# A graph attention kernel: seven row tiles are transposed by DMA as half words instead of by TensorE, and the search steps over adj are placed differently

## The chip, the core and the metric

The kernel runs on one core of a Trainium2 chip. The time is device microseconds (us) of one execution of the whole program. A core has a matrix engine (TensorE, in the profile PE; its weight loads are PEld), three engines for element work (VectorE = DVE, ScalarE = ACT, GpSimd = POOL), a sync engine (SP) whose work here is to issue DMAs, and 16 DMA engines that all queues share. Each engine works through its own list of instructions in order and waits on semaphores for the others.

## What is computed

One layer of attention over a graph of 2708 nodes with 1024 features, in float32. `adj` is a matrix of zeros and ones with a one at a chance of 0.0014771, so that a node has four neighbours on average.

```python
h = jnp.maximum(_layernorm(x, axis=-1), 0.0)
q = h @ W_q.T + b_q;  k = h @ W_k.T + b_k;  v = h @ W_v.T + b_v
z = scale * (q @ k.T) * adj
z = jnp.where(z == 0.0, -10000.0, z)
out = x + relu(softmax(z, axis=1) @ v)
```

## The kernel before

**What is multiplied.** The kernel never forms k or v. It folds W_q and W_k into one matrix M, makes rows q = h M + bias, fetches for each node the rows h of its neighbours, takes scores as dot products of q with them, and adds the neighbours' rows up, weighted by the softmax: u. Then out = x + relu(u W_v + b_v). So there are two large products, both of 128 rows by 1024 with 1024x1024: h by M ("q units") and u by W_v ("o units").

**Row tiles.** There are 22 tiles of 128 rows, the last with 20. Rows are sorted by their number of neighbours, in two parts: tiles 0 to 10, and 11 to 21. The sort needs the lists of neighbours ("keys") of all rows of its part, and it yields a table (`tab`) by which rows are scattered and gathered from then on.

**The search for neighbours.** A tile of adj (128x2708, 1354 KB) is loaded by SP (L317) into one of three buffers, tile t into buffer t % 3. ACT passes over it once (`counted`, L324, output `sized`) to sum it, which is a check value; DVE searches it for the positions of the ones (`found`, L334, four or five instructions over 128x685 or less), and then makes the list of keys from the positions (`listed`, L346 to L352), one time per batch of up to four tiles. Tiles 20 and 21 are batches of their own. The next tile for a buffer can load when both ACT's pass and DVE's search of the tile before are through. The search steps stand between the matmul blocks, in a table `steps_at` that maps (unit, position) to a string: `p` is ACT's pass alone, `f` is search and, at a batch's end, list, `i` is search alone, `j` is list alone, `e` is all of them. `c` stands for the counts of a part, `o` for its sort. The counts of the second part stand at unit 3, position 2, its sort at unit 3, position 3 (L604 `hot` on DVE, then two small matmuls at L615 and L617).

**A unit.** A unit is a pair of tiles, multiplied with seven block products in place of eight, of sums of quarter blocks: per unit the operands a11, a12 (of the first tile), a22, a21 (of the second), and sums s1 to s4 of them, against quarters of M (or W_v) and their sums T. A block is four matmuls of 128x512 in `add_block` (L909). In `multiply` the blocks come in the order s2, a12, s4, s3, then a11 and s1 of the **next** unit (`opened`), then a22; `after(0)` to `after(6)` run what stands between them. The sums that are c12, c22 (p or q rows, L1020 for o units) are made on DVE from PSUM, c11 and c21 on ACT. Units n = 0 to 9 are q pairs; n = 10 to 19 are o pairs: (8,7), (6,5), (4,3), (2,0), (1,9), (15,14), (13,12), (16,17), (20,10), (18,19). Tile 11 is left over and is multiplied alone at the end.

**How a row tile comes to stand as an operand.** The features must lie on the partitions, so each 128x1024 tile is transposed. `half_turned` (L357 to L360) has PE transpose four blocks of 128x128 into one PSUM bank `pt`, twice a tile. `blocks` (L640 to L680) has ACT copy a11, a12 and a22 out of PSUM (L649) and DVE make s1 and s3 from a21 in PSUM, s2 and s4 from SBUF (L653). In `after`, the first tile of the next pair is turned at position 0 and the second at position 2. For tile 11, `turned` (L362 to L367) does the same into one tile `T_alone`.

**The attention stream.** From unit 5 on, `attention` runs as a stream of steps beside the matmuls, `advance(share)` after each block: scores of the next tile on DVE (L790, 128x1024 with a sum), exp on ACT (L806), coefficients on DVE (L834), the first product coef times g on ACT (L835), the other products added on DVE one after another (`sums`, L843). The rows g are gathered by POOL (L545). The order of tiles is 8, 7, 6, 5, 4, 3, 2, 0, 1, 9, 15, 14, 13, 12, 16, 17, 20, 10, 18, 19, 11. Tiles 10 and 20 hold nodes without neighbours and take a row sum of h besides. If two tiles' neighbours fit together (`ahead`), two score steps of the next tile come ahead of a tile's weights. The finished u either stays in SBUF (`held`, when it is used within two units) or is stored by POOL to `u_dram`, from where SP loads it again (`load_rows`, L1103) two units ahead of its use.

**What sets the order.** DVE's order is written out by hand throughout, ACT's and POOL's by hand up to unit 5 and by the compiler's scheduler after that; SP's queue takes adj loads, row loads, weights for the o units and small tail transfers in their order.

Of the kernel before, what the change touches and what calls it, by code (L numbers as in the profile page):

```python
# [10 lines left out]
FT = mybir.dt.float32  # L11
U32 = mybir.dt.uint32
I32 = mybir.dt.int32
U16 = mybir.dt.uint16
AF = mybir.ActivationFunctionType
ALU = mybir.AluOpType
AX = mybir.AxisListType

P = 128
NB = 512  # L20
# [12 lines left out]
FAR = 20.0  # L33
WIDE = 8
LIGHT = 4
ROOT = 32
BATCHES = ((0, 3), (4, 7), (8, 11), (12, 15), (16, 19), (20, 20), (21, 21))

# [19 lines left out]
def tile_preln_masked_attention(  # L58
# [12 lines left out]
    nc = tc.nc  # L71
    N, D = x.shape
    DC = D // P
# [4 lines left out]
    FULL = N // P  # L78
# [4 lines left out]
    K = slot_counts(EARLY * P, EARLY) + slot_counts(N - EARLY * P, FULL - EARLY) + [0]  # L83
# [7 lines left out]
    dram = ctx.enter_context(tc.tile_pool(name="dram", bufs=1, space=bass.MemoryType.DRAM))  # L91
# [3 lines left out]
    q_dram = dram.tile([EARLY * P, D], FT, name="q_dram")  # L95
    q_late = dram.tile([(FULL - EARLY) * P, D], FT, name="q_late")
    u_dram = dram.tile([FULL * P, D], FT, name="u_dram")
    m_dram = dram.tile([2, 2, P, 4, NB], FT, name="m_dram")
    tv_dram = dram.tile([4, P, 4, NB], FT, name="tv_dram")
    bp_dram = dram.tile([1, D], FT, name="bp_dram")  # L100
# [54 lines left out]
    t = 0  # L155
    while t < NT:
# [4 lines left out]
        t = e  # L161
# [24 lines left out]
    def row_tile(name):  # L186
        return work.tile([P, D], FT, tag="row", name=name, bufs=ROWS)
# [166 lines left out]
    def half_turned(xt, s):  # L354

        pt = psum.tile([P, 4, P], FT, tag="tp", name="pt")
        for c in range(4):  # L357
            k = s * 4 + c
            nc.tensor.transpose(pt[:, c, :], xt[:, k * P:(k + 1) * P], ident)  # L359
        return pt  # L360

    def turned(xt, name):  # L362

        hT = work.tile([P, D], FT, tag="hT", name=f"T_{name}", bufs=2).rearrange("p (c q) -> p c q", q=P)
        for s in range(DC // 4):
            nc.scalar.copy(hT[:, s * 4:(s + 1) * 4, :], half_turned(xt, s))
        return hT  # L367

    ordered = ExitStack()
    ordered.enter_context(tc.manual_schedule(engines={mybir.EngineType.Activation, mybir.EngineType.DVE}))  # L370
# [17 lines left out]
    with tc.tile_pool(name="w", bufs=1, side="left") as wp:  # L388
# [73 lines left out]
        if True:  # L462
# [7 lines left out]
            for o in range(DC):  # L470
# [6 lines left out]
                else:  # L477
                    k = o - H
# [60 lines left out]
    def small(name):  # L539
        return half.tile([P, NB], FT, tag="half", name=name, bufs=14)  # L540
# [98 lines left out]

    behind = []  # L640

    def blocks(xa, xb, eng=None):


        ops = {}

        def held(name, bank):
            ops[name] = small(name).rearrange("p (c q) -> p c q", q=P)
            nc.scalar.copy(ops[name], bank)  # L649

        def put(name, a, b, op, eng=None):
            ops[name] = small(name).rearrange("p (c q) -> p c q", q=P)
            step = (eng or nc.vector).tensor_tensor(ops[name], a, b, op=op)  # L653
            if eng is None:
                behind.append(step)

        def upper():
            held("a11", half_turned(xa, 0))
            held("a12", half_turned(xa, 1))

        def lower():
            held("a22", half_turned(xb, 1))
            a21 = half_turned(xb, 0)
            put("s1", ops["a22"], a21, ALU.add)
            put("s3", ops["a11"], a21, ALU.subtract)
            put("s2", ops["s1"], ops["a11"], ALU.subtract, eng)
            put("s4", ops["a12"], ops["s2"], ALU.subtract, eng)

        return ops, upper, lower
# [3 lines left out]
    def banks_for(row):  # L673

        return_ = []
        for h in range(NH):
            return_.append(psum.tile([P, NB], FT, tag="acc", name=f"ps{h}"))
            nc.scalar.copy(return_[h], row[:, h * NB:(h + 1) * NB])
        return return_

    def natural_rows(n):
# [15 lines left out]
    nc.vector.tensor_scalar(large[:, 0:1], large[:, 0:1], 10000.0, None, op0=ALU.is_gt)  # L697
    nc.vector.tensor_scalar(large[:, 1:2], large[:, 1:2], 250000.0 / D, None, op0=ALU.is_gt)

    steps_at = {(0, 0): "s4-5 e9", (0, 1): "r4 +0 +1 +2 f10", (0, 3): "p10 i11", (0, 4): "j11 a4 p11", (0, 5): "h4 +3 s6-7 e12",  # L700
# [3 lines left out]
    steps_ahead = {(2, 2): "o s10"}  # L704

    slots, free = [], []
# [132 lines left out]
    def sums(t):  # L839
        u, coef = us.pop(t)  # L840
        for s in range(0 if t in EMPTY else 1, K[t]):
            fill()
            chained(lambda: nc.vector.scalar_tensor_tensor(  # L843
                u, g_of[t][s], coef[:, at[t][s]:at[t][s] + 1], u, op0=ALU.mult, op1=ALU.add))
            free.append(g_of[t][s])
            yield 1.3
        fill()
        g_of.pop(t)
        if near(t):
            held[t] = u  # L850
        else:
            nc.gpsimd.dma_start(u_dram[t * P:(t + 1) * P, :], u)
        done.add(t)

    def attention(order):
        for t in order[:2]:
            ask(t)

        fill()
        yield 0.0  # L860
        with tc.issue_after(chain[-1].ins):
            for lo, hi in parts:
                nc.vector.tensor_scalar(valid[:, lo:hi], ptab.bitcast(U32)[:, lo:hi, 0:SLOTS], float(N) - 0.5, NONE,
                                        op0=ALU.is_lt, op1=ALU.max)
        free.extend(slots[:8])
        fill()
        yield 0.0
        fetch(order[0])
        after = order[1:] + [None, None]
        yield from scores(order[0], after[0])  # L870
        for i, t in enumerate(order):
            nxt = after[i]
            ahead = nxt is not None and K[t] + K[nxt] <= HIGH + 1
            part = scores(nxt, after[i + 1]) if nxt is not None else iter(())
            if ahead:

                for _ in range(2):
                    yield next(part, 0.0)
            weights(t)
            yield 0.6  # L880
            if ahead:
                yield from part
            yield from sums(t)
            yield from part
# [9 lines left out]
    def near(t):  # L894

        return t == alone or any(t in unit[1:] for unit in units[:now[0] + 3] if unit[0] == "o")
# [190 lines left out]
    o_pairs = [(order[i], order[i + 1]) for i in range(0, FULL - 1, 2)]  # L1087
    alone = order[-1]
    units = [("q",) + p for p in q_pairs] + [("o",) + p for p in o_pairs]

    def load_rows(unit):
        kind, *pair = unit
        rows = []
        for t in pair:
            if t in held:
                rows.append(held.pop(t))
                continue
            rows.append(row_tile(f"{kind}r_{t}"))
            if kind == "q":
                gather(rows[-1], h_dram[:, :], t, SLOTS, P)  # L1100
            else:
                assert t in done, (t, done)
                nc.sync.dma_start(rows[-1], u_dram[t * P:(t + 1) * P, :])  # L1103
        return rows
# [42 lines left out]
    for n, unit in enumerate(units):  # L1147
# [10 lines left out]
        def after(i):  # L1158
# [18 lines left out]
            if nxt is not None:  # L1177

                if n == FIRST - 1 and i in (0, 2):
                    single_turned(i // 2)  # L1180
                if i == (3 if n in (0, FIRST - 1) else 0):
                    ops_of[n + 1] = blocks(*rows_of[n + 1], nc.gpsimd if n + 1 < FIRST - 1 else None)
                    if n != FIRST - 1:
                        ops_of[n + 1][1]()
                if n != FIRST - 1 and i == (4 if n == 0 else 2):
                    ops_of[n + 1][2]()
                    rows_of.pop(n + 1)
                    if n == last_q - 1:
                        all_rows()
                if i == 3:  # L1190
                    if n == FIRST - 1:
                        single["banks"] = banks_for(bp_sb)
                    else:
                        banks_of[n + 1] = banks_for(bp_sb)
                if i == 4 and n + 2 < FIRST:
                    natural_rows(n + 2)
                if i == (2 if n == FIRST else 4) and n + 2 >= FIRST and n + 2 < len(units) and n + 2 not in rows_of:
                    while units[n + 2][0] == "o" and not done.issuperset(units[n + 2][1:]):
                        advance(1.0)
                    rows_of[n + 2] = load_rows(units[n + 2])  # L1200
# [6 lines left out]
            if nxt is None and i == 1:  # L1207
                while alone not in done:
                    advance(1.0)
                r, = load_rows(("o", alone))  # L1210
                single["turned"] = turned(r, "alone")
            if nxt is None and i == 3:
                single["banks"] = banks_for(bp_sb)
            if n == last_q - 1 and i == 4:

                nc.sync.dma_start(bp_sb, bv.to_broadcast([P, D]))
                nc.vector.tensor_sub(bp_sb[:, NB:], bp_sb[:, NB:], bp_sb[:, :NB])
# [238 lines left out]
```

## Time and profile before

| | |
|---|---|
| median of 3 runs | 669.54 us (668.49 to 670.58) |
| profiled execution, its own time | 670.24 us |
| its span, first to last instruction | 668.4 us |
| granted TensorE clock, mean | 0.993 |
| ACT busy | 264.3 us, 40% |
| POOL busy | 401.4 us, 60% |
| share of the chain that ended last: PE | 79% |
| the same: DMA 5%, DVE 5%, POOL 4%, ACT 2%, issue 5% | |
| gathers of rows g (L545), 104 of them | 125.1 us of POOL |
| scores (L790), 92 | 112.6 us of DVE, 1.22 us each |
| sums (L843), 77 | 98.8 us of DVE, 1.28 us each |
| ACT's passes over adj (L324), 22 | 54.2 us, 2.46 us each |
| ACT's copies out of the transposes (L649), 60 | 33.2 us |
| DMA, 193.24 MB | mean 289 GB/s over the span |

A line of PE, DVE or ACT in a timeline gives the start and the duration in us, the engine, the line of the kernel, the operation, output<-input, shapes, and the number of instructions in a row; in square brackets stands the idle time of the engine just ahead and what ended it. A line of the waits gives engine and tile, the engine and tile that ended the wait, then the sum in us, the count, and the mean. Matmuls of one group overlap: the distance from one group's start to the next one's is what a group costs, 3.43 us for a block of four matmuls that shows 3.60 us in its line.

### The profile page before, as it was taken

To read this page: it belongs to the slowest core of one execution; us is meant where nothing else is said; L and a number is where in the kernel's file an instruction comes from. 1 tells how busy PE (TensorE), PEld (TensorE's weight loads), DVE (VectorE), ACT (ScalarE), POOL (GpSimd) and SP (SyncE) were. 2 spreads that over 40 slices of the span, in tenths; PEclk is the share of its full clock that TensorE was granted. 3 is DMA by queue.
4 is the path that set the end of the run, shared out by engine and by line. 5 is a ranking of instruction groups with operands and counts; after the bars stand their busy time and mean duration, and the time that the engine had idled before them with its cause. 6 is when DMAs were issued, how large, how long until landed. Compare 5 with 4: busy or idle time off the path is not lost.

```text
span 668.4 us, 6383 instructions
## 1 busy us (share of the span) xinstructions
PE 653.6 (98%) x1768; PEld 334.0 (50%) x1768; DVE 526.0 (79%) x1014; ACT 264.3 (40%) x395; POOL 401.4 (60%) x396
## 2 busy tenths in 40 slices
PE   7999999999998999999999999999999999999994
PEld 4777766444543444444444444444444444444441
DVE  5999879999887403988887999798798989989221
ACT  3467985765654212332241232432332433322200
POOL 2559991666476763775656365574674877873331
PEclk9999999999998999999999999999999999999998
DMA  8997989599575996897899999998997799895631
GB/s 345 408 360 259 371 302 377 220 400 340 207 222 171 343 374 219 276 393 240 312 312 351 382 417 390 305 302 252 325 299 193 235 296 364 220 278 170 147 121 66
DMA packets 62164, 193.24 MB, mean 289 GB/s; under 512 B 9689, under 2 KB 10041, under 8 KB 61226
## 3 DMA queue, kind: packets, MB, share of 16 engines
q0 software_dynamic: 34464, 109.25, 49.8%
q1 hardware_dynamic: 26650, 80.37, 32.5%
q10 hardware_dynamic: 1008, 3.15, 1.2%
q8 instruction: 16, 0.26, 0.2%
q14 instruction: 26, 0.21, 0.1%
HBM read 160.85 MB, written 44.93 MB: 308 GB/s over the span
## 4 chain that ended last, share of the span: by engine, by line
PE 79%; issue 5%; DMA 5%; DVE 5%; POOL 4%; ACT 2%; POOLq 0%; SPq 0%; DVEq 0%; ACTq 0%
PE ps L909 35%; PE psy L909 24%; PE ps_y L418 6%; PE ps_x L418 4%; PE ps_z L418 4%; PE pt L359 4%; POOL g L545 2%; DMA out_dram<-y,tab 2%; DMA adj<-in_adj_dram 2%; DVE junk L790 1%; DVE at L334 1%; POOL y L1008 1%; ACT sized L324 1%; DVE u L843 1%; DMA wlow<-in_wq_dram 1%
## 5 line engine op out<-in xcount | busy, mean ns | idle before, releaser
L545 POOL DMA_INDIRECT g<-h_dram,tab x104 | 125.1, 1203 | 54.5 <-issue 22.5
L909 PE MATMUL ps<-M,a 128*128 128x512 f32 x320 | 144.1, 593 | 0.1
L909 PE MATMUL psy<-wlow,s 128*128 128x512 f32 x320 | 144.1, 592 | 0.0
L790 DVE SCALAR_TENSOR_TENSOR junk<-g,pq 128x1024 uint8<-128x1024 f32 x92 | 112.6, 1224 | 2.3 <-DMA g<-h_dram,tab 0.4
L843 DVE SCALAR_TENSOR_TENSOR u<-g,coef,u 128x1024 f32<-128x1024 f32 x77 | 98.8, 1283 | 8.9 <-ACT u L835 7.3
L909 PEld LDWEIGHTS ps<-M,a 128*128 128x128 f32 x320 | 59.3, 190 | 68.0 <-issue 67.2
L909 PEld LDWEIGHTS psy<-wlow,s 128*128 128x128 f32 x320 | 59.2, 190 | 67.2 <-issue 67.2
L334 DVE FIND_INDEX8 at<-ones,adj 128x8 uint32<-128x685 f32 (+1 forms) x88 | 74.4, 866 | 0.0
L909 PE MATMUL ps<-M,s 128*128 128x512 f32 x160 | 73.6, 603 | 0.0
L909 PE MATMUL psy<-wlow,a 128*128 128x512 f32 x160 | 72.1, 593 | 0.4 <-DVE p L1020 0.4
L909 PE MATMUL ps<-wlow,s 128*128 128x512 f32 x160 | 71.9, 592 | 0.0
L324 ACT ACTIVATE sized<-adj 128x2708 uint8<-128x2708 f32 (+1 forms) x22 | 54.2, 2463 | 5.1 <-DMA adj<-in_adj_dram 5.0
L909 PEld LDWEIGHTS ps<-M,s 128*128 128x128 f32 x160 | 30.9, 194 | 38.4 <-issue 38.4
L1008 POOL DMA_INDIRECT y<-in_x_dram,tab x19 | 34.0, 1788 | 26.7 <-ACT y L1025 14.9
L909 PEld LDWEIGHTS psy<-wlow,a 128*128 128x128 f32 x160 | 30.2, 190 | 39.2 <-issue 34.6
L909 PEld LDWEIGHTS ps<-wlow,s 128*128 128x128 f32 x160 | 30.4, 190 | 38.3 <-issue 38.3
L259 POOL TENSOR_TENSOR hsum<-hsum,x 128x1024 f32<-128x1024 f32 (+1 forms) x17 | 40.3, 2370 | 0.3
L653 DVE TENSOR_TENSOR s<-a,pt 128x512 f32<-128x512 f32 x40 | 25.6, 681 | 15.5 <-ACT a L649 6.9
L649 ACT COPY a<-pt 128x512 f32<-128x512 f32 x60 | 33.2, 593 | 9.5 <-remote 3.7
L547 POOL DMA_INDIRECT pq<-q_dram,tab x11 | 14.6, 1329 | 33.5 <-DVE junk L790 16.3
L744 POOL DMA_INDIRECT out_dram<-y,tab x21 | 24.9, 1186 | 15.4 <-DMA y<-in_x_dram,tab 7.7
L545 POOL DMA_INDIRECT M<-h_dram,tab x20 | 27.0, 1350 | 10.1 <-issue 4.9
(236 smaller groups left out, 887.1 us busy)
## 6 DMA issues: line engine op xcount, KB each, us to landing
adj<-in_adj_dram SPq DMA_DIRECT2D x21, 1354.0 KB
x<-in_x_dram SPq DMA_DIRECT2D x21, 512.0 KB
h_dram<-x POOLq DMA_DIRECT2D x21, 512.0 KB
u_dram<-u POOLq DMA_DIRECT2D x14, 512.0 KB
or<-u_dram SPq DMA_DIRECT2D x14, 512.0 KB
q_late<-q SPq DMA_DIRECT2D x10, 512.0 KB
pq<-q_late POOLq DMA_DIRECT2D x10, 512.0 KB
g<-in_wv_dram SPq DMA_DIRECT2D x16, 256.0 KB
```

The source lines that it names most:

```text
L259: nc.gpsimd.tensor_add(hsum[:n], hsum[:n], xt[:n])
L324: nc.scalar.activation(sized[:n], a[:n, :, :PW], AF.Abs, accum_out=total[:n, t:t + 1])
L334: nc.vector.max_index(at[:n, t - first_t, g, :], ones[:n, 0:8], a[:n, g, :])
L359: nc.tensor.transpose(pt[:, c, :], xt[:, k * P:(k + 1) * P], ident)
L418: mm = nc.tensor.matmul(bank, a_tile(o + H * a[0], a[1], i), b(o), start=first and o == 0, stop=(o == H - 1), skip_group_check=True)
L545: return nc.gpsimd.indirect_dma_start(out=dst, out_offset=None, in_=src, in_offset=off, bounds_check=N - 1, oob_is_err=False)
L649: nc.scalar.copy(ops[name], bank)
L653: step = (eng or nc.vector).tensor_tensor(ops[name], a, b, op=op)
L790: chained(lambda: nc.vector.scalar_tensor_tensor(junk, g_of[t][s], 1.0, tq[t], op0=ALU.mult, op1=ALU.mult, accum_out=zall[:, t, s:s + 1]))
L843: chained(lambda: nc.vector.scalar_tensor_tensor(u, g_of[t][s], coef[:, at[t][s]:at[t][s] + 1], u, op0=ALU.mult, op1=ALU.add))
L909: mm = nc.tensor.matmul(bank, a[:, c, :], b[:, c, :], start=False, stop=(c == 3), skip_group_check=True)
L1008: return nc.gpsimd.indirect_dma_start(out=y[:n], out_offset=None, in_=x, in_offset=off, compute_op=ALU.add)
```

## The change

Three things are done.

**Seven row tiles are no longer transposed on PE.** `TURNED = 3` names the last three o pairs, and with the tile left over they are the tiles 16, 17, 20, 10, 18, 19 and 11 (`turning`). The DMA transposes elements of two bytes, and the rows are float32, so a tile is first split: at the end of `sums`, ACT copies the high and the low half words of u, taken as 128x2048 numbers of 16 bits, into the two halves of a new row tile. It is held (16, 17, 10, 11) or stored by POOL in a new `u_split` (20, 18, 19). In `load_rows`, SP issues one transposing DMA for such a tile, in place of taking the held tile or loading from `u_dram`; it gives sixteen blocks of 128x128 half words. In `blocks_turned`, which stands for `blocks`, ACT joins high and low half words again into a11, a12, a22 and now a21 too, two copies for each, and DVE makes s1 to s4 all from SBUF. For these pairs the first tile is joined at position 3 of the unit before and the second at position 4, where they were turned at 0 and 2. For tile 11 the transposing DMA is issued in the last unit at position 1, and joined at position 4 into `T_alone`.

**Search steps are moved.** ACT's passes over the adj tiles 16, 17 and 18 each stand a step earlier; the search of 19 stands one step earlier and its list by itself behind it; the list of batch 8 to 11 stands one step later.

**A bound on the score steps.** `ahead` takes at most one step less than the next tile has scores, where it took two.

```diff
+TURNED = 3
+    u_split = dram.tile([FULL * P, 2 * D], U16, name="u_split")
...
+    def words_joined(dst, turned, lo, hi):
+        words = dst.bitcast(U16).rearrange("p (k w) -> p k w", w=2)
+        for w in (1, 0):
+            nc.scalar.copy(words[:, :, w], turned[:, (1 - w) * D + lo:(1 - w) * D + hi])
+    def blocks_turned(ta, tb):
...
+        def joined_half(name, turned, s):
+            half = small(name)
+            words_joined(half, turned, s * NB, (s + 1) * NB)
...
+        def upper():
+            joined_half("a11", ta, 0)
+            joined_half("a12", ta, 1)
+        def lower():
+            joined_half("a22", tb, 1)
+            joined_half("a21", tb, 0)
+            put("s1", "a22", "a21", ALU.add)
+            put("s3", "a11", "a21", ALU.subtract)
+            put("s2", "s1", "a11", ALU.subtract)
+            put("s4", "a12", "s2", ALU.subtract)
...
-    steps_at = {... (0, 3): "p10 i11", (0, 4): "j11 a4 p11", (0, 5): "h4 +3 s6-7 e12",
+    steps_at = {... (0, 3): "p10 i11", (0, 4): "a4 p11", (0, 5): "j11 h4 +3 s6-7 e12",
-                (1, 6): "f16 c", (2, 1): "f17", (2, 2): "p16 a8", (2, 3): "r10 f18 p17 w h8",
-                (2, 4): "a10 p18", (2, 5): "f19 k10", ...
+                (1, 6): "f16 c p16", (2, 1): "f17", (2, 2): "p17 a8", (2, 3): "r10 f18 p18 w h8",
+                (2, 4): "i19 a10", (2, 5): "j19 k10", ...
...
@@ in sums(t), behind the last sum @@
+        kept_in = u_dram
+        if t in turning:
+            words = u.bitcast(U16).rearrange("p (k w) -> p k w", w=2)
+            u = row_tile(f"split_{t}").bitcast(U16)
+            kept_in = u_split
+            for w in (1, 0):
+                nc.scalar.copy(u[:, (1 - w) * D:(2 - w) * D], words[:, :, w])
...
@@ in attention() @@
-                for _ in range(2):
+                for _ in range(min(2, K[nxt] - 1)):
...
+    turning = {t for p in o_pairs[-TURNED:] for t in p} | {alone}
...
@@ in load_rows(unit) @@
+            if kind == "o" and t in turning:
+                rows.append(row_tile(f"{kind}r_{t}").bitcast(U16))
+                nc.sync.dma_start_transpose(rows[-1].rearrange("p (c r) -> p c r", r=P),
+                                            held.pop(t) if t in held else u_split[t * P:(t + 1) * P, :])
+                continue
...
@@ in after(i) @@
-                if i == (3 if n in (0, FIRST - 1) else 0):
+                by_dma = nxt[0] == "o" and nxt[1] in turning
+                if i == (3 if n in (0, FIRST - 1) or by_dma else 0):
...
-                if n != FIRST - 1 and i == (4 if n == 0 else 2):
+                if n != FIRST - 1 and i == (4 if n == 0 or by_dma else 2):
...
-                single["turned"] = turned(r, "alone")
+                single["row"], = load_rows(("o", alone))
...
+            if nxt is None and i == 4:
+                uT = work.tile([P, D], FT, tag="hT", name="T_alone", bufs=2)
+                words_joined(uT, single["row"], 0, D)
```

More of the change, by code (lines that the diff above doesn't have):

```diff
@@ L360, in half_turned @@
         return pt
[L362 to L367, printed above, removed]
     ordered = ExitStack()
@@ L640, in tile_preln_masked_attention, with put @@
     behind = []
+    def words_joined(dst, turned, lo, hi):
[3 more added lines that the diff above has]
+    def blocks_turned(ta, tb):
+        ops = {}
+        def joined_half(name, turned, s):
+            half = small(name)
+            words_joined(half, turned, s * NB, (s + 1) * NB)
+            ops[name] = half.rearrange("p (c q) -> p c q", q=P)
+        def put(name, a, b, op):
+            ops[name] = small(name).rearrange("p (c q) -> p c q", q=P)
+            nc.vector.tensor_tensor(ops[name], ops[a], ops[b], op=op)
+        def upper():
[8 more added lines that the diff above has]
+            put("s4", "a12", "s2", ALU.subtract)
+        return ops, upper, lower
     def blocks(xa, xb, eng=None):
@@ L698, in tile_preln_masked_attention @@
     nc.vector.tensor_scalar(large[:, 1:2], large[:, 1:2], 250000.0 / D, None, op0=ALU.is_gt)
-    steps_at = {(0, 0): "s4-5 e9", (0, 1): "r4 +0 +1 +2 f10", (0, 3): "p10 i11", (0, 4): "j11 a4 p11", (0, 5): "h4 +3 s6-7 e12",
+    steps_at = {(0, 0): "s4-5 e9", (0, 1): "r4 +0 +1 +2 f10", (0, 3): "p10 i11", (0, 4): "a4 p11", (0, 5): "j11 h4 +3 s6-7 e12",
                 (0, 6): "r6 f13", (1, 1): "f14", (1, 2): "p13 a6", (1, 3): "h6 s8-9 p14", (1, 4): "r8 p15 i15", (1, 5): "j15",
[2 rows of a table removed]
[2 rows of a table added]
     steps_ahead = {(2, 2): "o s10"}
@@ L851, in sums @@
         else:
-            nc.gpsimd.dma_start(u_dram[t * P:(t + 1) * P, :], u)
+            nc.gpsimd.dma_start(kept_in[t * P:(t + 1) * P, :], u)
         done.add(t)
@@ L1180, in after @@
                     single_turned(i // 2)
-                if i == (3 if n in (0, FIRST - 1) else 0):
-                    ops_of[n + 1] = blocks(*rows_of[n + 1], nc.gpsimd if n + 1 < FIRST - 1 else None)
+                by_dma = nxt[0] == "o" and nxt[1] in turning
+                if i == (3 if n in (0, FIRST - 1) or by_dma else 0):
+                    ops_of[n + 1] = blocks_turned(*rows_of[n + 1]) if by_dma else \
+                        blocks(*rows_of[n + 1], nc.gpsimd if n + 1 < FIRST - 1 else None)
                     if n != FIRST - 1:
                         ops_of[n + 1][1]()
-                if n != FIRST - 1 and i == (4 if n == 0 else 2):
+                if n != FIRST - 1 and i == (4 if n == 0 or by_dma else 2):
                     ops_of[n + 1][2]()
@@ L1209, in after @@
                     advance(1.0)
-                r, = load_rows(("o", alone))
-                single["turned"] = turned(r, "alone")
+                single["row"], = load_rows(("o", alone))
             if nxt is None and i == 3:
                 single["banks"] = banks_for(bp_sb)
+            if nxt is None and i == 4:
+                uT = work.tile([P, D], FT, tag="hT", name="T_alone", bufs=2)
+                words_joined(uT, single["row"], 0, D)
+                single["turned"] = uT.rearrange("p (c q) -> p c q", q=P)
             if n == last_q - 1 and i == 4:
```

2 rows, old and new, of the table steps_at are left out of this document.

## The prediction

> **What bounds the kernel.** I read the page first, then PE's waits, then the timelines of PE, DVE and ACT around the two places that the change touches.
>
> ```profile
> PE 653.6 (98%) x1768; PEld 334.0 (50%) x1768; DVE 526.0 (79%) x1014; ACT 264.3 (40%) x395; POOL 401.4 (60%) x396
> ```
>
> PE is busy in 98% of the span, so the time is what PE does plus its few waits, and 8.6 us after its last matmul. PE's waits, whole:
>
> ```profile
> PE ps_y L453 <- POOL hsum L119: 2.8, 1, 2.8
> PE ps_in L615 <- DVE hot L604: 2.2, 1, 2.2
> PE ps_x L418 <- DMA wlow<-in_wq_dram: 0.8, 1, 0.8
> PE psy L909 <- DVE p L1020: 0.4, 1, 0.4
> ```
>
> Two belong to the change. The 2.2 us is the sort of the second part, before which the keys of the last adj tiles must be found. PE's timeline there (start, duration, idle before it):
>
> ```profile
> 198.22 3.60 PE L909 MATMUL ps<-M,a 128*128 128x512 f32 x8
> 204.03 0.57 PE L615 MATMUL ps_in<-hot,before 128*128 128x198 f32 x2 [2.22 <-DVE hot L604]
> 204.44 0.58 PE L617 MATMUL ps_all<-hot,ones 128*128 128x198 f32 x2
> 204.82 5.25 PE L909 MATMUL ps<-M,s 128*128 128x512 f32 x8
> 209.91 3.60 PE L909 MATMUL psy<-wlow,s 128*128 128x512 f32 x8
> ```
>
> The wait costs more than itself: the eight records after it last 5.25 us where every other such group lasts 3.60. The stretch from 204.03 to 209.91 is 5.88 us; the same work elsewhere is 0.67 (first sort, 170.89 to 171.56) + 3.43 = 4.10, so 1.78 us more, with the clock at 0.97 in the window from 200 to 250 and 1.00 in its neighbours. Why the keys were late, from the chain of waits:
>
> ```profile
> 178.97 2.50 ACT sized L324 x2
> 181.83 10.94 DMA adj<-in_adj_dram
> 192.95 3.48 DVE at L334 x5
> ```
>
> There are three adj buffers, so tile 20 loads when ACT's pass over 17 ends (181.3), and the load takes 11 us, until DVE can search 20 at 192.95.
>
> The other place is the end. PE's transposes of a row tile, and its one short wait:
>
> ```profile
> 549.68 1.04 PE L359 MATMUL pt<-ident,u 128*128 128x128 f32 x8
> 550.55 3.60 PE L909 MATMUL psy<-wlow,s 128*128 128x512 f32 x8
> 568.59 3.60 PE L909 MATMUL ps<-wlow,s 128*128 128x512 f32 x8
> 572.55 3.70 PE L909 MATMUL psy<-wlow,a 128*128 128x512 f32 x8 [0.36 <-DVE p L1020]
> ```
>
> A transposed tile takes PE 0.87 us from start to start (549.68 to 550.55), a block of four matmuls 3.43. The 0.36 at 572.55 says that DVE, which runs with next to no pause from 510 to 620, is only just in time for PE:
>
> ```profile
> 569.43 1.15 ACT L835 ACTIVATE u<-g,coef 128x1024 f32<-128x1024 f32 x1 [1.11 <-DVE coef L834]
> ```
> ```profile
> 570.61 1.28 DVE L843 SCALAR_TENSOR_TENSOR u<-g,coef,u 128x1024 f32<-128x1024 f32 x1 [1.22 <-ACT u L835]
> 571.81 0.69 DVE L1020 TENSOR_TENSOR p<-psy,p 128x512 f32<-128x512 f32 x1
> ```
>
> DVE waits for ACT's first product of tile 19, sums, and then makes the add that PE waits for. Whatever ACT puts ahead of that product moves PE.
>
> All times below are on the clock of this execution: span 668.4, its own time 670.24, 0.70 above the median of 669.54.
>
> **Part 1, adj passes and keys: -4.0 us.** In the new order ACT's pass over 16 stands ahead of two evictions, right after ACT's store at 167.8; it ends at 170.5 (2.65 a pass) and not 175.2. The evictions then end at 171.7; PE, which needs their banks for its next transposes, has matmuls ahead of these in the new order, so PE pays nothing. Pass 17 ends at 176.1, not 181.3; pass 18 at 182.6, not 191.4. Load 20 starts 5 us earlier and, at the 11 us of the row above, lands by 187.2. DVE after its search of 18 (180.65) and an add: search 19 (3.4) to 184.7; its adj, issued at 170.6, needs 9 us as before. The c22 add now comes behind that search, ending at 185.3; PE needs it at 189.6. List 3.2 to 188.5, search 20 to 191.9 (load there by 187.2, 1.3 us to spare), its list 1.1, search 21 3.4, list 1.1, counts 1.5: hot is there by 199.3. PE asks at 198.22 + 3.43 = 201.65. The wait of 2.22 goes, and with it the slow group of 1.78: 4.0. POOL's sums of h go behind its table writes, the writes start earlier, and nothing else of POOL is on PE's path; next late is nothing within 2 us. What follows hangs on PE (DVE's own waits until 510 are mostly for PE), so all of it moves with PE; I count the 4.0 to the end.
>
> The Trainium skill (TensorE: Matmul & The Clock Gate, Part 1) says that the clock halves after an idle window of about 3.4 us and comes back after as long a busy one. Here 2.2 us of idling was enough, and 1.78 lost is half of such a window, so the size agrees and the threshold doesn't; by the page's threshold a wait like those below would cost only itself.
>
> **Part 2, transposes off PE: -6.1.** Seven row tiles (16, 17, 20, 10, 18, 19 and 11) x 0.87. The old 0.36, with the 0.1 around it, is replaced too: -0.5.
>
> **What it adds on ACT.** Per tile two split copies of 128x1024 and, joining, four of 512 (two of 1024 for tile 11). No row shows a copy with a step of two half words; the nearest are copies of the same count, 1.15 and 0.58. Bounds: no less than the 1.04 of an ACT pass that writes bytes, up to twice, 2.3, if the step halves the rate; I take 1.15 and 0.58, so 4.6 us a tile, 32 us in all, less 11 evictions of 0.57. ACT is 40% busy, so the sum hides; its place in the queue does not.
>
> - Pair (15,14): a score (1.27) now stands on DVE ahead of the p add that ended at 545.65, and the exp of tile 20 stands on ACT behind the split of 17. The add ends near 547.3; PE wants it at 546.24. **+1.1.**
> - Pair (13,12): 18's last sum ended at 568.85 and, as four DVE passes (2.5) move behind it, ends at 566.3. ACT's split of 18 then takes 2.3, the product for 19, which is now behind it, 1.15, DVE's first sum for 19 1.3, and only then comes s1 (0.65): 571.7. PE is ready for s1 at 568.59 - 1.74 + 1.1 = 567.95 and finds one matmul (0.86) to put in front. **+2.9.** This is longer than the 2.22 above, so I add a slow group of the same size: **+1.8.**
> - Later pairs: DVE is 1.8 us later than before, but s1 and the p adds come within a microsecond ahead of PE. 0.
>
> **The transposing DMAs.** SP issues seven of 512 KB. No row shows one. Bounds: whole 512 KB transfers in the chain of waits took 4.0 us (a gather) to 6.2 (a scatter); upwards, the new DMA writes 2048 runs of 256 bytes, and the eleven table scatters, 128 rows each, follow each other every 1.26 us, which makes 20 us. I take 6, the nearer row by bytes. With 6 the first six are a pair ahead of their use (tile 17: split by 544.2, joined from 561.7; 17 us). Tile 11 is tight: its last sum ends near 622, the split near 624.5, then the DMA, then ACT has two joins, an eviction, a bank and the u2 copy (4.1) before PE's s3 block, 638.84 before and 638.0 now. So there is room for 9 us. In SP's queue the small tail store and load stand around it; both have 10 us and more.
>
> **Sum.** -4.0 - 6.1 - 0.5 + 1.1 + 2.9 + 1.8 = -4.8: 665.4 in the profiled execution's terms, **664.7 us** against the median. Its own range, from the copies and that group: 662.5 to 667.
>
> **Rivals.**
>
> 1. *No new waits.* ACT runs split and product in the gaps so that s1 is in time: -4.0 - 6.1 - 0.5, 659.0. For it: DVE gets back two waits of 1.22 for products. Against: the order puts s1 behind 19's sum. 0.12.
> 2. *The keys are not earlier*, as load 20 shares the engines with load 19 and lands later than 190: -0.8 only, 668.7. For it: the loads take 9 to 11 us for 1.35 MB at a DMA share of 0.76. Against: 2.3 us to spare. 0.12.
> 3. *Tile 11 is late by a few us*: a transposing DMA of 9 to 17 us, or transposes that slow the gathers at DMA shares of 0.84 to 1.00 from 520 to 600. Each us over 9 is one at the end: 665 to 673. 0.10.
> 4. *Slower: the transposing DMA takes some 20 us.* Mechanism: ACT's queue stands at tile 11's join, with the eviction, the bank and u2 behind it, and PE at s3. From 9 us on it costs a us per us: 11 + 2.5 for tile 17, 678; if the seven also go one after another (7 x 20 from 533.7, so 673.7, + 4.1 + 29.6 to the span's end, - 4.0, and 1.1 from span to median's terms), 704. For it: the runs of 256 bytes. Against: 512 KB moves in 4.0 to 6.2 us. 0.18.
>
> The Trainium skill has rules on both sides of rival 4. VectorE: DVE Perf Modes, The three transpose paths, gives 1309 ns for one 128x128 of two bytes: sixteen to a row tile, an estimate of 21 us if one follows another. DMA: Bandwidth & Descriptors, Latency and other measured facts, gives 261 GB/s, an estimate of 2 us. No run here shows either yet.
>
> **Chances.** Forecast 0.48, rivals 0.12, 0.12, 0.10, 0.18. A measurement here tells 0.3% (2.0 us) from no change. Faster by more: 0.48 + 0.12 + 0.03 of rival 3 = 0.63. Within: 0.12 + 0.04 = 0.16. Slower: 0.18 + 0.03 = 0.21. The range leaves out rival 4 alone: 659 to 673.
>
> **What would show it.** Part 1: PE's wait for hot gone, and the group behind it at 3.60. Part 2: no transposes of PE after 550, seven fewer. The added waits: PE idle of 2 to 4 us before the s1 block of pair (16,17), released by DVE s, with a split copy and a product just before on ACT. The DMA: seven SP issues, ACT's T_alone join starting at most 9 us after its split, and no PE wait for u2. Wrong if ACT's split copies last over 1.5 us, if the join of tile 11 starts later than that, or if PE still waits for hot.

## The result and the profile after

The changed kernel takes **692.08 us** (median of 6 runs, 681.59 to 707.8), the kernel before 669.79 in the same series (668.49 to 670.58): a ratio of 1.0241, with a 95% interval of 1.0205 to 1.0277. The ratio leaves out the three runs over 1.5% above the fastest and rests on 681.59, 685.3 and 691.74, so the profiled execution, whose time is explained below, is the longest of those kept. The forecast was 664.7, between 659 and 673. The profiled execution took 691.74, the one of before 670.24: 21.5 us more.

The first line of the profile's page, to be held against that of before:

```profile
PE 649.7 (94%) x1712; PEld 328.8 (48%) x1712; DVE 529.2 (77%) x1014; ACT 288.5 (42%) x424; POOL 399.1 (58%) x396
```

PE does 56 instructions less (seven tiles of eight transposes), and its share falls from 98% to 94%: it now waits. PE's waits, whole (engine, line and tile, what ended the wait; us in total, times, and the longest one, which the explanation of the views ahead calls the mean):

```profile
PE ps L945 <- ACT psy L958: 17.3, 1, 17.3
PE ps L945 <- DVE s L655: 9.4, 1, 9.4
PE ps_y L448 <- POOL hsum L121: 2.8, 1, 2.8
PE pt L361 <- DVE sort L614: 1.3, 1, 1.3
PE ps_x L413 <- DMA wlow<-in_wq_dram: 0.9, 1, 0.9
```

The wait for `hot` and the one for `p` are gone. New are 1.3 us at the first sort and two long waits, before the pairs (16,17) and (20,10). PE's timeline at the second sort and at both long waits (start, duration, then idle before in brackets):

```profile
202.99 0.57 PE L610 MATMUL ps_in<-hot,before 128*128 128x198 f32 x2
203.40 0.50 PE L612 MATMUL ps_all<-hot,ones 128*128 128x198 f32 x2
203.74 3.60 PE L945 MATMUL ps<-M,s 128*128 128x512 f32 x8
...
581.77 2.08 PE L945 MATMUL ps<-M,a 128*128 128x512 f32 x2 [17.26 <-ACT psy L958]
583.64 5.00 PE L945 MATMUL ps<-wlow,s 128*128 128x512 f32 x8
588.48 3.60 PE L945 MATMUL psy<-wlow,a 128*128 128x512 f32 x8
...
617.73 5.10 PE L945 MATMUL ps<-wlow,s 128*128 128x512 f32 x8 [9.35 <-DVE s L655]
```

The eight matmuls behind the second sort last 3.60, as forecast. Behind each long wait they last 5.0 and 5.1. What these waits hang on is seen on the other engines. ACT ahead of 581.77, and ahead of 617.73:

```profile
569.90 0.76 ACT L641 COPY a<-or 128x512 uint16<-128x512 uint16 x1 [12.83 <-DMA or<-split]
573.90 1.15 ACT L864 ACTIVATE u<-g,coef 128x1024 f32<-128x1024 f32 x1 [3.24 <-DVE coef L863]
...
581.14 0.57 ACT L958 COPY psy<-ps 128x512 f32<-128x512 f32 x1
...
613.30 0.76 ACT L641 COPY a<-or 128x512 uint16<-128x512 uint16 x1 [12.98 <-DMA or<-split]
```

DVE at the same place, SP's issues, and the two longest pieces of the chain of waits behind 500 us:

```profile
570.82 1.23 DVE L819 SCALAR_TENSOR_TENSOR junk<-g,pq 128x1024 uint8<-128x1024 f32 x1 [16.66 <-DMA pq<-q_late]
```
```profile
530.79 23.65 SPq L1134 DMA_TRANSPOSE or<-split  x2
```
```profile
545.69 25.11 DMA pq<-q_late
...
587.26 26.02 DMA or<-split
```

Ahead of the first wait two things are late at once. The transposing DMA of tile 17, which SP issues at 540.7 as the split ends, is there at 569.9, 29 us later, and ACT's queue stands at its join for 12.83, with `psy`, PE's next bank, behind it. And the plain load of a q tile, issued by POOL at 545.69, takes 25.11 us, so that DVE's scores stand for 16.66. The second wait hangs on the transposing DMA of tile 10, issued at 587.26 and there at 613.28: ACT stands at its join for 12.98, and the joins and s follow. The prediction's rival 4 looked for this at tile 11; there the DMA ran with few others and ACT's join began 8 us after the split (647.5 to 655.6), without a wait of PE.

The 21.5 us add up, nearly: the two waits are 26.6; the groups behind them lost 1.0, 1.4 and 1.5 against 0.86 and 3.43 from start to start (581.77 to 583.64, 583.64 to 588.48, 617.73 to 622.67), 30.5 in all; the steps gave 2.7, with the 1.3 at the first sort taken off already (PE's last transposes common to both start at 528.20 before and at 525.46 after), the transposes 6.1, the old wait for p 0.5. 30.5 - 9.3 = 21.2.

### The profile page after: what moved, and what is told of

The parts are those of the page before. It is cut to its first block, busy times and chain, and to the rows that moved or that the text cites. A ratio compares the mean times of both kernels' runs of the same rounds, so it can differ in the third digit from the quotient of the medians.

```text
span 690.0 us, 6299 instructions
## 1 busy us (share of the span) xinstructions
PE 649.7 (94%) x1712; PEld 328.8 (48%) x1712; DVE 529.2 (77%) x1014; ACT 288.5 (42%) x424; POOL 399.1 (58%) x396
## 4 chain that ended last, share of the span: by engine, by line
PE 74%; DMA 14%; DVE 6%; ACT 2%; issue 2%; POOL 1%; POOLq 0%; ACTq 0%; DVEq 0%
PE ps L945 34%; PE psy L945 22%; PE ps_y L413 6%; PE ps_x L413 4%; PE ps_z L413 4%; DMA or<-split 4%; DMA pq<-q_late 4%; PE pt L361 3%; DMA adj<-in_adj_dram 2%; DVE at L336 2%; DMA g<-h_dram,tab 2%; DMA or<-u_split 1%; DVE u L872 1%; DMA wlow<-in_wq_dram 1%; ACT sized L326 1%
## 5 line engine op out<-in xcount | busy, mean ns | idle before, releaser
L945 PE MATMUL ps<-M,a 128*128 128x512 f32 x320 | 145.6, 596 | 17.3 <-ACT psy L958 17.3
L945 PE MATMUL ps<-wlow,s 128*128 128x512 f32 x160 | 74.8, 612 | 9.4 <-DVE s L655 9.4
L945 PE MATMUL ps<-M,s 128*128 128x512 f32 x160 | 71.9, 592 | 0.0
L682 DVE TENSOR_TENSOR s<-a,pt 128x512 f32<-128x512 f32 x34 | 21.7, 680 | 14.7 <-ACT a L678 14.7
L678 ACT COPY a<-pt 128x512 f32<-128x512 f32 x51 | 28.2, 593 | 6.4 <-PE pt L361 6.4
L540 POOL DMA_INDIRECT M<-h_dram,tab x20 | 24.2, 1208 | 11.4 <-DMA h_dram<-x 4.6
```

Source lines behind the costliest of these rows:

```text
L540: return nc.gpsimd.indirect_dma_start(out=dst, out_offset=None, in_=src, in_offset=off, bounds_check=N - 1, oob_is_err=False)
L945: mm = nc.tensor.matmul(bank, a[:, c, :], b[:, c, :], start=False, stop=(c == 3), skip_group_check=True)
```

## Experiments

The theory after the result: **the transposing DMA beside gathers**; it is late, and it makes others late. The rivals: **the order** (splits and joins in ACT's queue, as in the forecast's added waits), and **late operands alone** (only the joins wait, the other transfers are none the worse).

**plain_rows**: the transposing DMA becomes a plain one.

```diff
-                nc.sync.dma_start_transpose(rows[-1].rearrange("p (c r) -> p c r", r=P),
-                                            held.pop(t) if t in held else u_split[t * P:(t + 1) * P, :])
+                nc.sync.dma_start(rows[-1], held.pop(t) if t in held else u_split[t * P:(t + 1) * P, :])
```

> The changed kernel with each transposing DMA replaced by a plain one of the same 512 KB from the same place; it leaves the transposes of seven tiles out. Theory 'DMA' (both long PE waits, 17.3 and 9.4 us, come from the transposing): both gone, 659 to 666 us. Rival 'order' (they come from where splits and joins stand in ACT's queue and behind DVE's sums): they stay, over 680 us.

Measured 662.14 us, a ratio of 0.9907 (0.9871 to 0.9943). Two of PE's waits are left from the two long ones:

```profile
PE ps L945 <- ACT psy L958: 0.9, 1, 0.9
PE ps L945 <- DVE s L655: 0.3, 1, 0.3
```

So the order is not it: splits, joins and queues are the same here, and 30 us are gone. The bytes are the same, too. All of the loss comes with the transposing by DMA.

**alone_dma**, transfers alone.

> A kernel of a few transfers only, it leaves out the whole computation and writes copies of x's first rows: in turn a plain 512 KB copy inside SBUF, transposing DMAs of 512, 256 and 128 KB, one of 512 KB from HBM, three of 512 KB at once, four gathers of 512 KB alone, four gathers beside a transposing DMA, four beside a plain copy. Theory 'shared' (a transposing DMA is short by itself and long, and makes others long, only beside gathers): about 8 us for 512 KB alone, as tile 11's took in the changed kernel from issue (647.6) to join (655.6), half that for half, and the four gathers beside it twice as long as alone. Theory 'slow by itself': 18 to 26 us alone too, as the others took, and little change of the gathers.

512 KB took 4.4 us from issue to landing (14.6 to 19.0; in crowd, below, 4.12 to 8.54), 256 KB 3.2, 128 KB 2.5, three in a row 9.4. "Slow by itself" falls. The transposing DMA beside four gathers took 5.9 and these no longer than without, but it was through before they had begun; that part says nothing.

The Trainium skill (VectorE: DVE Perf Modes, The three transpose paths) has 1309 ns for one 128x128 of two bytes, an estimate of 21 us for sixteen one after another; 4.4 were measured. The Trainium skill (DMA: Bandwidth & Descriptors, Latency and other measured facts) has 261 GB/s, an estimate of 2 us; three in a row took 3.1 each, which is 169 GB/s.

**crowd** ties the transposing DMA to the landing of the first of 16 queued loads.

> A kernel of transfers only, it leaves out the whole computation and writes copies of x's first rows: 16 plain loads of 512 KB from HBM queued at once by POOL, then the same with a transposing DMA of 512 KB from SP issued when the first has landed, then the same with a plain 512 KB copy issued there. Theory 'turns' (each DMA engine takes one packet from each queue in turn, 4096 bytes in 159 ns for a load and 256 bytes in 18 ns for the transposing DMA, which has 128 of these per engine): the transposing DMA lasts as long as the loads still queued, about 20 us where it takes 4.4 alone, the plain copy, with 8 packets per engine, 3 to 6 us, and the 16 loads become some 2.5 us longer. Theory 'shared by bytes': the transposing DMA takes some 9 us, like the plain copy beside the loads. Theory 'crossbar blocks': the loads become longer by much more than 4.4 us.

DVE's timeline (the first line shows the first load landed, the second the transposing DMA, issued at 43.49):

```profile
43.31 0.15 DVE L54 COPY src<-row 128x1 f32<-128x1 f32 x1 [5.59 <-DMA row<-in_x_dram]
64.69 0.15 DVE L54 COPY src<-dst 128x1 f32<-128x1 f32 x1 [21.22 <-DMA dst<-src]
```

21.2 us for what takes 4.4 alone, and the transfers by queue in a window inside it (47 to 59; q0 the loads, q1 the transposing DMA):

```profile
DMA packets 2434, 4.88 MB, mean 407 GB/s; under 512 B 1316, under 2 KB 1316, under 8 KB 2434
...
q0 software_dynamic: 1249, 4.58, 93.4%
q1 hardware_dynamic: 1185, 0.30, 11.1%
```

Packets go nearly one for one: 1249 of the loads' queue, 4096 bytes but for some 130 tiny ones, against 1185 of 256 bytes. A tile is 2048 packets by this kind of DMA, and 128 by a plain one, so it needs sixteen times the turns. At 1185 in 12 us, 2048 take 20.7 us, which is nearly the whole 21.2. The loads lost little: 4.58 MB in 12 us, 4.92 without. "Shared by bytes" (9 us) and "crossbar blocks" (the transposing itself holds up the loads) fall for plain loads. The plain copy took 9.3 us, above the 3 to 6 expected: turns are not the whole wait of a DMA that comes behind a full queue. No run moves packets of 256 bytes without transposing, so that the size of the packets alone does it is argued here, not shown.

**steps_only**, the kernel before with the new `steps_at`.

> The kernel before with the moved search steps alone. The prediction's part 1: -4.0, 665.8 us. By the changed kernel's trace, in which PE is 2.7 us ahead at 525 and has a new wait of 1.3 at the first sort: -2.7, 667.1 us. A loss of part 1: over 670.

666.95 us, 0.9958 (0.9944 to 0.9971): 3.3 less than the 670.23 beside it, between the two expectations. The profile has the new wait at the first sort, 1.2, and not the old one.

**alone_only**: `turning = {alone}`.

> The changed kernel with tile 11 alone transposed by DMA, the six tiles of pairs on PE as before. Theory 'shared': tile 11's DMA runs when the gathers are over, lands some 8 us after its split and within the room of 9: 666 us (-2.7 for the steps, -0.9 for one tile's transposes). Theory 'slow by itself': 18 to 26 us, 9 to 17 over the room: 676 to 684.

666.81 us, 0.9943 (0.9921 to 0.9965), as expected: no wait of PE behind 600. Against steps_only it is no measurable gain.

**half_words**: one half of the words transposed.

```diff
-            nc.scalar.copy(words[:, :, w], turned[:, (1 - w) * D + lo:(1 - w) * D + hi])
+            nc.scalar.copy(words[:, :, w], turned[:, lo:hi])
...
+                nc.sync.dma_start_transpose(rows[-1][:, :D].rearrange("p (c r) -> p c r", r=P), src[:, :D])
```

> The changed kernel with only the high half words transposed, 256 KB in place of 512 per tile and joined twice, so that it leaves out half of the transposing. Theory 'turns': half the packets, so half the time beside gathers, 9 to 15 us; the two PE waits (17.3 and 9.4) shrink to under half: 664 to 675. A fixed cost per transposing DMA: both stay, 685 or more.

681.05 us, 1.0143 (1.0106 to 1.018): above the range of "turns". But the two waits of PE did shrink, the first to 35%, the second to 60%:

```profile
PE ps L945 <- ACT psy L958: 6.1, 1, 6.1
PE ps L945 <- DVE s L655: 5.6, 1, 5.6
```

A fixed cost per transposing DMA falls. Half the packets are half the bytes as well, so this run doesn't tell these two apart.

**turn_only**, the old steps with the rest of the change.

> The changed kernel with the search steps where they were. The steps gave 2.7 to 3.3 us in steps_only; if the two parts don't touch each other, this is 3 us slower than the changed kernel, 688 to 696; rival: the steps shift the stream so that the transposing DMAs meet the gathers differently, and the time differs by 10 us either way.

690.47 us, 1.0238 (1.0155 to 1.0321), runs from 681.7 to 722.5: too wide to tell whether the parts simply add.

**turned1** and **turned2**: `TURNED = 1`, `TURNED = 2`.

> TURNED = 1: tiles 18, 19 and 11 by DMA, 16, 17, 20 and 10 on PE. The two long waits of the changed kernel stood before pairs (16,17) and (20,10); if each is made by that pair's own transposes beside gathers, both go here: 663 to 668. If any transposing DMA beside tile 11's gathers is 15 to 25 us long and late, there is a wait of 5 us or more before pair (18,19): 670 to 680.

> TURNED = 2: tiles 20, 10, 18, 19 and 11 by DMA, 16 and 17 on PE. turned1 measured 664.1. If the second long wait of the changed kernel (9.4, before pair (20,10)) is made by that pair's own transposes beside the gathers of tile 11: it stays, 669 to 675. If it came only from the stream being late after the first wait: gone, 662 to 664.

turned1 takes 664.14 us, 0.9904 (0.9874 to 0.9934), with no wait of PE behind the sorts. turned2 takes 681.28, 1.0143 (1.0075 to 1.0212), over the 669 to 675 expected. In its profile, of an execution of 690.78 that is the longest of the four (the shortest took 675.83), PE waits 7.32 us before (20,10) and 15.52 before (18,19), both for `s`. The first has no transposes of (16,17) ahead of it, so the wait before (20,10) is made by its own. The second is new: SP's two transposing DMAs of 18 and 19 take 30.75 us to issue where turned1's take 8.31. In the changed kernel these two take 17.77 and PE does not wait for them.

**dead_turns**, **dead_behind** and their control **plain_12** (the cut is of dead_behind): joins read plainly loaded rows, and the seven transposing DMAs are issued besides, into a tile that nobody reads.

```diff
+                unread.append((src, nc.sync.dma_start(rows[-1], src)))
...
+        for src, _ in unread:
+            with tc.issue_after(unread[-1][1].ins):
+                nc.sync.dma_start_transpose(spare.rearrange("p (c r) -> p c r", r=P), src)
```

> The kernel of plain_rows (662.1 us), whose joins read plainly loaded rows, so that seven tiles are not transposed, with the seven transposing DMAs issued besides, right behind a pair's plain loads, into a tile that nobody reads (one of the 13 gather buffers). Theory 'late operand' (PE waits only because joins wait for transposes): 661 to 667, as plain_12. Theory 'others late' (they also hold up gathers and rows of q, on which scores and sums wait): at least half of the 26.7 us of waits stays, 675 to 690.

> The control for dead_turns: plain_rows with 12 gather buffers in place of 13, seven tiles not transposed. Within 2 us of plain_rows, 660 to 665.

> As dead_turns (joins read plainly loaded rows, so seven tiles are not transposed; the seven transposing DMAs are issued besides and nobody reads them), but with each pair's transposing DMAs behind both of the pair's plain loads on SP. Theory 'late operand alone': 661 to 667, as plain_12 (662.0). Theory 'others late too': rows of q and gathers still land 15 to 25 us after issue, DVE's scores wait, and 672 to 690.

plain_12 takes 662.03 (0.9883, 0.9859 to 0.9906). dead_turns takes 698.16 (1.0448, 1.0403 to 1.0494), but there the scheduler had put the plain loads behind the unread DMAs in SP's queue. dead_behind, without that fault, takes **714.65** (1.0553, 1.0525 to 1.0581). PE's and DVE's longest waits, from an execution of 720.27:

```profile
PE ps L945 <- ACT psy L958: 40.4, 1, 40.4
PE ps L945 <- DVE s L655: 12.9, 2, 10.1
```
```profile
DVE u L872 <- ACT u L864: 23.3, 3, 21.8
DVE junk L819 <- DMA pq<-q_late: 20.6, 1, 20.6
DVE y L1081 <- DMA y<-in_x_dram,tab: 13.8, 1, 13.8
```

and three pieces of its chain of waits between 540 and 610:

```profile
541.03 31.06 DMA y<-in_x_dram,tab
...
574.49 27.05 DMA pq<-q_late
...
605.11 18.28 DMA u_split<-split
```

No operand is transposed by DMA here, and it is the slowest of all: "late operands alone" falls. Other transfers of POOL's queue are late by 20 us and more. (Part of the 714 is the experiment's own: a split is needed for two DMAs, and ACT waits 19.3 us for a row buffer until the unread one has read it. Of the 52.6 us over plain_12 this leaves some 33; the changed kernel lies 29.9 over plain_rows.)

**crowd_kinds** and **crowd_kinds2**: which transfers are held up.

> Transfers only, the whole computation is left out: 12 indirect gathers of 512 KB by POOL, alone and with a transposing DMA of 512 KB issued behind the fourth; the same with 12 accumulating gathers, and with 12 indirect scatters to HBM. Beside plain loads the transposing DMA took 21.2 us and the loads none longer. Theory 'turns' alone: here too the transposing DMA lasts as long as the queue beside it is full (10 to 15 us for 12, since POOL issues one every 1.25 us) and the 12 transfers are at most 3 us longer. Theory 'kinds': with accumulating gathers or scatters, as the kernel has them between its gathers, packets wait for each other, and the 12 transfers become 5 us or more longer.

> Transfers only, the whole computation is left out: 12 indirect transfers of 512 KB by POOL, alone and then with a transposing DMA of 512 KB issued when the first has landed; four kinds: gathers, accumulating gathers (2.5 us each alone in crowd_kinds, where a gather takes 1.3), scatters, and the three by turns. Theory 'turns' alone: the transposing DMA lasts as long as the queue beside it is full, longest beside accumulating gathers (128 packets per engine of 18 ns, each behind one of 328 ns), and the 12 are at most 3 us longer. Theory 'kinds': beside accumulating gathers or scatters the 12 become 5 us or more longer.

In crowd_kinds the transposing DMA ran before the others began, at 4.5 us; it shows only that an accumulating gather, which adds to what stands in its destination, takes 2.5 us where a gather takes 1.3. crowd_kinds2, by DVE's timeline, from the landing of the first of 12 to that of the last:

| 12 transfers of | alone | beside one transposing DMA | that DMA itself |
|---|---|---|---|
| gathers | 15.9 us | 26.8 | 23.2 |
| accumulating gathers | 28.8 | 49.1 | 42.7 |
| scatters | 15.5 | 18.2 | 9.5 |
| the three by turns | 22.6 | 24.5 | 12.7 |

The row of the gathers, in three lines of that view: first gather, transposing DMA, last gather.

```profile
31.59 0.15 DVE L88 COPY row<-row 128x1 f32<-128x1 f32 x1 [5.75 <-DMA row<-in_x_dram,idx]
...
55.21 0.15 DVE L59 COPY src<-dst 128x1 f32<-128x1 f32 x1 [18.61 <-DMA dst<-src]
...
58.34 0.15 DVE L92 COPY row<-row 128x1 f32<-128x1 f32 x1 [0.91 <-DMA row<-in_x_dram,idx]
```

One transposing DMA costs 12 gathers 10.9 us and 12 accumulating gathers 20.3, far over its own 4.4; plain loads, scatters and the three by turns little. "Turns" alone, 3 us at most, falls for gathers. "Kinds" holds for accumulating gathers alone; it falls for scatters, and for the three by turns (1.9 us), which mix the kinds as the kernel's queue does. Beside gathers the packets themselves last longer: from 38 to 54 us the transposing DMA's take 48 ns each (1350 in 25.2% of the 16 engines' time), beside plain loads 18 (1185 in 11.1% of 12 us), and the gathers' take 194 (974 in 73.7%) where they take 151 alone (1284 in 100.8% of 12 us). Why gathers suffer and plain loads of the same packets don't, no run shows.

**turned1_list**: turned1, with the list of batch 8 to 11 at (0, 4) again.

> turned1 (664.1 us) with the list of batch 8 to 11 back in its old place. If the new wait of the first sort comes from that list standing later on DVE: the wait goes, 662 to 663. If it comes from the search of 16 and 17: stays, 664.

663.23 us, 0.9904 (0.9888 to 0.9921). PE's wait at the first sort is gone from the profile; a new one of 0.5 for a q add stands in its place. That alone doesn't lay the wait on the moved list: plain_rows, plain_12 and dead_behind have the list in its new place and no such wait either. DVE and PE in the changed kernel:

```profile
149.10 0.09 DVE L336 MATCH_VALUE_LOAD at<-ones,adj 128x8 f32 x1 [3.27 <-DMA adj<-in_adj_dram]
...
173.09 0.35 DVE L614 COPY sort<-ps_all 128x198 f32<-128x198 f32 x1
```
```profile
171.19 1.02 PE L945 MATMUL ps<-M,a 128*128 128x512 f32 x2
173.49 0.66 PE L361 MATMUL pt<-ident,x 128*128 128x128 f32 x4 [1.28 <-DVE sort L614]
```

and DVE in plain_rows, with the same steps and no wait:

```profile
147.57 0.09 DVE L336 MATCH_VALUE_LOAD at<-ones,adj 128x8 f32 x1 [1.52 <-DMA adj<-in_adj_dram]
...
171.55 0.35 DVE L614 COPY sort<-ps_all 128x198 f32<-128x198 f32 x1
```

The wait goes with a load of adj. In the seven profiles of kernels with the new place of the list that have the wait, the load is there at 148.7 to 150.8, in the three that lack it at 147.6 to 147.8. In turn_only, with all old steps, it is there at 149.11 and DVE reads the sort at 173.13, but PE's transposes run at 171.85, ahead of that, and wait for nothing. So the new steps make these transposes wait for the sort to be read, and a late load then costs up to 2.0 us; why the load is late in some executions is open. turned1 and turned1_list both take 1% less than the kernel before; between the two, the times don't decide.

## Why the prediction was wrong

- **Part 1, -4.0**: -2.7 in the profile, -3.3 by steps_only. The mechanism was right: no wait for hot (PE asked at 202.99), the group behind it at 3.60. What failed is the step "PE, which needs their banks for its next transposes, has matmuls ahead of these in the new order, so PE pays nothing": in that new order the transposes behind these matmuls wait until DVE has read the first sort's banks, 1.3 us here. In plain_rows, where the load of adj is early, they don't, and PE's last common transposes start at 523.89, 4.3 before: there the 4.0 came out.
- **Part 2, -6.1 and -0.5**: held by the count (56 instructions less, no wait for p). plain_rows lies 4.8 us under steps_only, with the added waits of the next point inside.
- **Added waits, +1.1, +2.9 and +1.8**: mis-sized. In plain_rows, where only they are left, the s block of pair (15,14) ends 0.15 late and the blocks at the seam to (16,17) lose 1.7 (559.35 to 565.33, less 4.29). The waits were 0.9 at ACT's bank and 0.3 at s1, and no slow group followed (3.54 for 3.43). The split took 1.99 for two copies where 2.3 was taken; four joins took 2.6 where 2.3 was taken.
- **The transposing DMA, "I take 6, the nearer row by bytes"**: the step that failed. Alone it takes 4.4, under the value taken. Beside gathers it took 29, over the 20 set as the upper bound, against a cover of 17 us ("tile 17: split by 544.2, joined from 561.7"); tile 10's took 26. The prediction counted packets for the bound and then chose by bytes; by packets (2048 against 128) it would have been the other end.
- **"The first six are a pair ahead of their use"** failed with it, and so did rival 4's place: it looked at tile 11, where the gathers are over. Its chain was right (ACT's queue stands at the join, the bank and PE behind it), but its terms are those of tile 11 and of seven DMAs one after another; that 692 lies in its 678 to 704 is luck.
- **Transposes that slow the gathers** stood in rival 3 with 0.10 and a few us. dead_behind shows that a loss of the change's size comes about with no operand transposed by DMA, even without its own 19.3 us. How the changed kernel's loss is shared between its late operands and its late other transfers, no run shows.

What stays open: why gathers are held up, and plain loads and a mixed queue hardly; why the pair (18,19) costs 15.5 us in turned2's profile and nothing in turned1 or the changed kernel; and why the changed kernel's runs spread over 26 us where those of before spread over 2.

## What to carry over

A DMA that moves small packets is not priced safely by its bytes: count its packets too, and measure it with what will be in flight beside it at that time. A transfer that is hidden behind a busy stage can still cost by what it does to the other transfers of that stage: look at what gathers the same window holds before moving work from an engine to the DMA. Against the moved steps alone (666.95), the same edit gained 2.8 us for the last pair and the last tile, where the gathers are nearly over, and lost 25 for three pairs and the last tile.

## What the runs showed of the hardware

- A transposing DMA of 512 KB took 4.4 us alone, 21.2 beside queued plain loads, 23.2 beside gathers, 42.7 beside accumulating gathers, and it made the 12 gathers 10.9 us and the accumulating ones 20.3 us longer.
- Its 256-byte packets went nearly one for one with 4096-byte packets of plain loads (1185 to 1249 in 12 us); beside gathers it was 1350 to 974 in 16 us.
- SP's issue of one took 2.1 us alone and 10.6 beside loads; SP's queue stands for that time.
- PE's clock: the waits of 2.2, 9.4 and 17.3 us were followed by groups at a granted clock of 0.71 that lost 1.8, 1.5 and 1.4 us (behind the longest, two matmuls ahead at 0.50 lost 1.0 more). In turned2 7.3 us of waiting cost 2.9 and 15.5 cost 2.1. The loss does not grow with the wait in these five.
